# One deformable-convolution and attention kernel: image 0's sampling in turn with the other images' offsets

## The chip, the core and the metric

The kernel runs on one core of one Trainium2 chip. The metric is device time in microseconds for one launch, as the median of several runs. One more execution was recorded by the hardware profiler, and all lines of the profile are of that execution.

A core has five engines that matter here. TensorE (PE in the profile, its weight loads PEld) multiplies matrices and also transposes. VectorE (DVE) does elementwise work and reductions. ScalarE (ACT) does activations and copies. GpSimd (POOL) does elementwise work and issues indirect transfers. SyncE (SP) issues transfers. Each engine carries out its own instructions in order; engines wait for each other at semaphores.

## The reference

Four images of 64 x 64 tokens and 256 channels in fp32 pass through two layers.

```python
# layer 0
g  = _gn(x)                                   # group norm, 32 groups
xp = g @ in_w + in_b                          # what is sampled
x1 = silu(batchnorm(depthwise3x3(g)))         # 256 channels
offset = x1 @ off_w + off_b                   # 8 groups x 9 points x (x, y)
mask   = softmax((x1 @ mask_w + mask_b).reshape(N, H, W, 8, 9), -1)
# each of the 9 points of a group is read bilinearly at its own place plus its offset,
# in xp with a border of one zero token, weighted by the mask, and the nine are added
x  = x + (samples * mask).sum(-1) @ out_w + out_b
# layer 1, on t = tokens of x
t = t + additive_attention(_ln_t(t))          # tanh(q[i] + k[j]) . Wa, softmax, weighted sum
t = t + half_capacity_ffn(_ln_t(t))           # feed forward for the upper half of the tokens
```

The offsets depend on the data, so where an image is read differs from token to token.

## The kernel before

The tokens of an image are cut into 32 tiles of 128. Layer 0 is computed in two stages that meet in memory outside the core.

**Offsets and weights** (`offsets_and_weights`, L263) is called once for all four images, in a scope of its own. For each image it has a *front* and then a loop over slabs; a slab is 8 tiles (`SLAB`), so there are four slabs an image.

- `front` loads the tokens (L336 on), turns them to channels on PE (L339), counts their statistics on DVE (L341), copies them into a padded image `xn` with ACT (L342) and normalises it there (L366). The front of the next image is stepped through within the slabs of this one.
- `convolution` computes the depthwise 3 x 3 convolution. Channel chunk 1 goes through PE as nine matmuls by diagonal matrices (L420), chunk 0 through DVE as nine multiply-adds (L432, L434). ACT applies batch norm and SiLU (L424, L435). A slab's convolution is issued ahead of the taps of the slab before.
- `taps` multiplies by the weights of offsets and masks (L444), DVE takes the result out of PSUM (L448) and begins the softmax (L456, L457).
- `window` ends the softmax (L463 to L465), makes three hat functions of each offset on ACT (L473 to L477), and the largest absolute offset of each token (L476). With these, DVE spreads the nine points' bilinear weights over a 5 x 5 window of fixed shifts: for each of 3 x 3 hats a product (`my` L483, `mxy` L486) and an addition into `w5` (L488), which POOL has set to zero (L480). PE turns the result (L497), ACT copies it (L499), and SP stores it in `wt`.
- `projection` computes `xp` for 16 image rows (L387, L392), stores it in `xp` (L398), and turns it back into a table of token pairs `tab` (L405 to L407). SP issues all these transfers.

Then the **pads**: zero rows above and below `xp` and `tab` of each image are stored from a zero tile `zm`, which POOL clears (L1393), by 24 transfers on SP (L1398, L1399).

Then **`sample_image(0, 6)`** (L672) runs alone. First `list_tokens` (L534) lists the tokens with an offset too large for the 5 x 5 window. For each of 4 token chunks of 1024 and 2 channel chunks, it loads a stretch of `xp` (`xs`, L687) and, for each of 25 shifts, a row of weights broadcast over partitions (`wb`, L692, 512 KB). DVE multiplies (L701) and adds (L709). With depth 6 there are 12 buffers for `wb` and two each for `xs`, `ac`, `prd`. In between, `exact_rows` (L567) computes listed tokens exactly with indirect transfers issued by POOL (L630). After each token chunk come the output projection (PE, L725), the bias on POOL (L729), the addition on DVE (L732) and the store of `t` (L733).

Then the loop over images: for each, attention's preparation (`attention_prep`, L787, which first loads `t` into `v`, L774) in turn with the feed forward of the image before and the sampling of the image after, and then attention itself. There, sampling has depth 1: two buffers of `wb`, one each of the others.

The order within a stage is set by the tile framework's scheduler, with priorities by the order in which the program issues instructions; `keep` holds an instruction to program order on its engine, and `pinned` does so for every operation of DVE that is called through it. The generators' `yield`s are the points at which the program goes from one stage to the other; `S.left` counts the steps that are left in sampling.

Of the kernel before, what the change touches and what calls it, by code (L numbers as in the profile page):

```python
# [45 lines left out]
def layers_kernel(ctx: ExitStack, tc: tile.TileContext, a, out: bass.AP):  # L46
# [207 lines left out]
    class Pinned:  # L254


        def __getattr__(self, name):
            op = getattr(nc.vector, name)
            return lambda *args, **kw: keep(op(*args, **kw))  # L259

    pinned = Pinned()

    def offsets_and_weights(images, slab, rows_bufs):  # L263

        ca = S.a_one
# [52 lines left out]
        diag = ca.tile([P, K2, P], F32, name="diag")  # L318
        for tap in range(K2):
            nc.vector.tensor_scalar(diag[:, tap], ident, dwk[:, 1, tap : tap + 1], None, ALU.mult)  # L320

        def front(n):

            xn = S.a_xn.tile([P, CC, PITCH, PITCH], F32, tag="xn", name="xn")
            for k in range(CC):
                for e in (0, PITCH - 1):
                    nc.gpsimd.memset(xn[:, k, e, :], 0.0)
                    nc.gpsimd.memset(xn[:, k, :, e : e + 1], 0.0)

            st = S.a_sm.tile([P, CC, 8, 6], F32, tag="st", name="st")  # L330
            for s in range(8):
                xt = S.a_ld.tile([P, 4, C], F32, tag="xt", name="xt")
                nc.sync.dma_start(
                    out=xt, in_=x_d[n, s * 512 : (s + 1) * 512].rearrange("(t p) c -> p t c", p=P)
                )
                for k in range(CC):  # L336
                    pt = S.a_t.tile([P, 4, P], F32, tag="pt", name="pt")
                    for t in range(4):
                        nc.tensor.transpose(pt[:, t, :], xt[:, t, k * P : (k + 1) * P], ident)  # L339
                    ptf = pt.rearrange("p t q -> p (t q)")  # L340
                    nc.vector.bn_stats(st[:, k, s, :], ptf)  # L341
                    nc.scalar.copy(  # L342
                        xn[:, k, 1 + 8 * s : 9 + 8 * s, 1 : 1 + W],
                        ptf.rearrange("p (r w) -> p r w", w=W),
                    )
                yield
            mv = S.a_sm.tile([P, CC, 2], F32, tag="mv", name="mv")
            for k in range(CC):
                nc.vector.bn_aggr(mv[:, k, :], st[:, k].rearrange("p s f -> p (s f)"))

            gavgf = gavg.rearrange("p a b -> p (a b)")
            pg = S.a_t.tile([P, CC], F32, tag="pt", name="pg")
            nc.tensor.matmul(pg, gavgf, mv[:, :, 0], start=True, stop=True)
            gm = S.a_sm.tile([P, CC], F32, tag="gm", name="gm")
            nc.vector.tensor_copy(gm, pg)
            gv = S.a_sm.tile([P, CC], F32, tag="gv", name="gv")
            nc.vector.tensor_sub(gv, mv[:, :, 0], gm)
            nc.vector.tensor_mul(gv, gv, gv)
            nc.vector.tensor_add(gv, gv, mv[:, :, 1])
            pg2 = S.a_t.tile([P, CC], F32, tag="pt", name="pg2")  # L360
            nc.tensor.matmul(pg2, gavgf, gv, start=True, stop=True)
            gr = inv_std(S.a_sm, pg2, CC, "gr")
            nc.vector.scalar_tensor_tensor(gm, gm, -1.0, gr, ALU.mult, ALU.mult)
            for k in range(CC):
                inner = xn[:, k, 1 : 1 + H, 1 : 1 + W]
                nc.scalar.activation(inner, inner, AF.Identity, bias=gm[:, k : k + 1], scale=gr[:, k : k + 1])  # L366
            xns[n] = xn
# [3 lines left out]
        for _ in front(images[0]):  # L371
            pass
        for at, n in enumerate(images):
            xn = xns.pop(n)
            after = front(images[at + 1]) if at + 1 < len(images) else iter(())
# [4 lines left out]
            def projection(s):  # L380
                xp = xps[s % len(xps)]
                for h in range(2):
                    for f in range(CC):
                        pm = S.a_m.tile([P, 8, W], F32, tag="pm", name="pm")
                        r0 = 16 * s + 8 * h
                        for k in range(CC):
                            nc.tensor.matmul(  # L387
# [9 lines left out]
                for f in range(CC):  # L397
                    nc.sync.dma_start(out=xp_d[n][f][:, q0 : q0 + 16 * MP], in_=xp[:, f, : 16 * MP])  # L398
                for o in range(0, 16 * MP, P):
                    m = min(P, 16 * MP - o)  # L400
                    pt = S.a_t.tile([P, 2, CC, P], F32, tag="pt", name="ptc")
                    tb = S.a_ld.tile([P, CC, GH, 2, CG], F32, tag="tb", name="tb")
                    for c in range(2):
                        for f in range(CC):
                            nc.tensor.transpose(pt[:m, c, f, :], xp[:, f, o + c : o + c + m], ident)  # L405
                        nc.scalar.copy(tb[:m, :, :, c, :], pt[:m, c].rearrange("p f (e g) -> p f g e", g=GH))
                    nc.sync.dma_start(out=tabw[q0 + o : q0 + o + m], in_=tb[:m].rearrange("p f g c e -> p (f g c e)"))  # L407


            x1s, raws = {}, {}  # L410

            def convolution(s):
# [3 lines left out]
                for o in range(0, slab * P, 512):  # L416
                    pc = S.a_m.tile([P, 8, W], F32, tag="pm", name="pc")
                    for tap in range(K2):
                        r = r0 + o // W + tap // 3
                        nc.tensor.matmul(  # L420
                            pc, diag[:, tap], xn[:, 1, r : r + 8, tap % 3 : tap % 3 + W],
                            start=(tap == 0), stop=(tap == K2 - 1),
                        )
                    nc.scalar.activation(  # L424
                        x1[:, 1, o : o + 512], pc.rearrange("p r w -> p (r w)"), AF.Silu,
                        bias=bnsh[:, 1:2], scale=bns[:, 1:2],
                    )
                acc = x1[:, 0].rearrange("p (r w) -> p r w", w=W)
                for tap in range(K2):
                    src = xn[:, 0, r0 + tap // 3 : r0 + tap // 3 + 2 * slab, tap % 3 : tap % 3 + W]  # L430
                    if tap == 0:
                        nc.vector.tensor_scalar(acc, src, dwk[:, 0, 0:1], None, ALU.mult)  # L432
                    else:
                        nc.vector.scalar_tensor_tensor(acc, src, dwk[:, 0, tap : tap + 1], acc, ALU.mult, ALU.add)  # L434
                nc.scalar.activation(x1[:, 0], x1[:, 0], AF.Silu, bias=bnsh[:, 0:1], scale=bns[:, 0:1])  # L435

            def taps(s):
                x1 = x1s.pop(s)
                raw = S.a_wk.tile([P, slab, 3 * GP], F32, tag="raw", name="raw")
                for t in range(0, slab, 2):  # L440
                    po = S.a_m.tile([P, 2, 3 * GP], F32, tag="pm", name="po")
                    for j in range(2):
                        for k in range(CC):
                            nc.tensor.matmul(  # L444
# [3 lines left out]
                    nc.vector.tensor_tensor(  # L448
# [7 lines left out]
                nc.vector.tensor_reduce(red, m3, AX.X, ALU.max)  # L456
                nc.vector.tensor_tensor(m3, m3, rbc, ALU.subtract)  # L457
# [3 lines left out]
            def window(s):  # L461
                raw, m3, red, rbc = raws.pop(s)
                nc.vector.tensor_reduce(red, m3, AX.X, ALU.add)  # L463
                nc.vector.reciprocal(red, red)
                nc.vector.tensor_tensor(m3, m3, rbc, ALU.mult)  # L465
# [10 lines left out]
                nc.vector.tensor_reduce(omax[:, n, s * slab : (s + 1) * slab], hat[:, 1], AX.X, ALU.max)  # L476
# [3 lines left out]
                nc.gpsimd.memset(w5, 0.0)  # L480
                for ey in range(3):
                    my = S.a_w1p.tile([P, slab, GP], F32, tag="my", name="my", bufs=2)
                    nc.vector.tensor_mul(my, raw[:, :, 2 * GP :], hat[:, ey, :, GP:])  # L483
                    for ex in range(3):
                        mxy = S.a_w1p.tile([P, slab, GP], F32, tag="mxy", name="mxy", bufs=2)
                        nc.vector.tensor_mul(mxy, my, hat[:, ex, :, :GP])  # L486
                        blk = w5[:, :, ex : ex + 3, ey : ey + 3]
                        nc.vector.tensor_tensor(  # L488
                            blk, blk, mxy.rearrange("p t (g i j) -> p (t g) i j", i=3, j=3), ALU.add
                        )  # L490

                w5t = w5.rearrange("p (t f g) i j -> p t f (g i j)", t=slab, f=CC)
                for t in range(0, slab, 4):
                    for f in range(CC):
                        pt = S.a_t.tile([P, 4, P], F32, tag="pt", name="ptw")
                        for j in range(4):
                            nc.tensor.transpose(pt[: GH * ND, j, :], w5t[:, t + j, f, :], ident)  # L497
# [3 lines left out]
                        nc.sync.dma_start(out=wt_d[n][f, :, o : o + 512], in_=wT[: GH * ND])  # L501

            ns = NT // slab
            convolution(0)
            for s in range(ns):
                if s + 1 < ns:
                    convolution(s + 1)
                taps(s)
                window(s)
                for i in range(s * (H // 16) // ns, (s + 1) * (H // 16) // ns):  # L510
                    projection(i)
                for _ in range(8 // ns):
                    next(after, None)
            for _ in after:
                pass
# [156 lines left out]
    def sample_image(n, depth=1):  # L672
# [8 lines left out]
        single = exact_rows(n, uf, exact)  # L681
        for c in range(L // CH):
            ac = S.dn.tile([P, CC, CH], F32, tag="ac", name="ac", bufs=min(depth, 2))
            for f in range(CC):
                xs = S.dn.tile([P, CH // W + 4, MP], F32, tag="xs2", name="xs2", bufs=min(depth, 2))
# [4 lines left out]
                for d in range(ND):  # L690
                    wb = S.dn.tile([P, CH], F32, tag="wb", name="wb", bufs=2 * depth)
# [6 lines left out]
                    else:  # L698
                        prt = S.dn.tile([P, CH], F32, tag="prd", name="prd", bufs=min(depth, 2))
# [5 lines left out]
                    S.left -= 1  # L705
                    own = S.gather and next(single, None)
# [5 lines left out]
                    while own:  # L712
                        own = next(single, None)
                        S.left -= 1
                        yield
            for i in range(0, CH // P, 2):
# [765 lines left out]
```

## Time and profile before

| what | value |
|---|---|
| median of 3 runs | 10574.97 us (10574.79 to 10576.85) |
| profiled execution | 10547.94 us |
| its span, from first to last recorded instruction | 10546.2 us |
| mean granted TensorE clock | 0.916 of full speed |
| DVE receives the first constant, `inw` (L269) | 30.10 us |
| first convolution on DVE (L432) | 55.16 us |
| first eviction of taps (L448) | 93.45 us |
| `zm` cleared (L1393) | 811.48 us |
| last pad issued (L1399) | 841.64 us |
| first product of image 0's sampling (L701) | 868.28 us |
| first load of `v` in attention's preparation (L774) | 1485.75 us |

The first part of the profile's page gives busy time by engine: PE 9022.3 us (86% of the span), DVE 8536.6 (81%), ACT 7374.7 (70%), POOL 5276.0 (50%). Its second part cuts the span into 40 equal slices of 264 us; a digit is the busy share of a slice in tenths, and the row `PEclk` the clock that the throttle granted to TensorE. The view of windows gives the same quantities for stretches that one chooses. The view of groups has one row for each kind of instruction: its line, engine, operation, output and inputs with their sizes, count; then busy time and the mean duration of one in ns; then idle time of the engine just before them, and what ended most of it. The timeline has one row for an instruction: its start, its duration in us, and in brackets how long its engine was idle before it and for what.

### The profile page before, as it was taken

Reading aid. Unit: us, or ns where it says so; the run is one execution under the profiler, and the core shown is the slowest. Engines: PE = TensorE matmul, PEld = TensorE weight load, DVE = VectorE, ACT = ScalarE, POOL = GpSimd, SP = SyncE. Lnnn points to the kernel's source line nnn. Section 1 sums busy time; section 2 is a strip of 40 time slices with the busy share of each in tenths; the row PEclk is TensorE's granted clock in tenths of the full one; section 3 lists DMA queues with packets and bytes.
Section 4 is the critical chain, followed back from the end, with each engine's and each line's share of the span. In section 5 each row is a group of like instructions: output and inputs, shape, how many; then the busy total and the mean of one; then the engine's idle time right before and its main releaser. Section 6 shows DMA issues by size and latency. Waiting matters only on the chain. (4 is left out here: it accounts for less than half of the span.)

```text
span 10546.2 us, 115935 instructions
## 1 busy us (share of the span) xinstructions
PE 9022.3 (86%) x38460; PEld 4384.6 (42%) x38460; DVE 8536.6 (81%) x13342; ACT 7374.7 (70%) x8389; POOL 5276.0 (50%) x3059
## 2 busy tenths in 40 slices
PE   7881039999999788999999689999999699999995
PEld 4541014444444343444444344444444344444443
DVE  7776879898989778989899679899898367777772
ACT  4450018888888537888888438888888379999991
POOL 0004207676555326767655327677555155555552
PEclk8995569999999888999999789999999799999997
DMA  3336642222212252212111342122111300000002
GB/s 120 108 137 184 206 164 70 61 67 61 70 64 74 95 168 63 52 54 58 53 55 51 115 154 53 53 53 55 52 57 43 101 13 9 10 8 7 7 5 75
DMA packets 381329, 766.00 MB, mean 73 GB/s; under 512 B 49104, under 2 KB 212592, under 8 KB 380688
## 3 DMA queue, kind: packets, MB, share of 16 engines
q1 hardware_dynamic: 324432, 678.78, 19.7%
q0 software_dynamic: 30144, 45.87, 2.8%
q10 hardware_dynamic: 26112, 33.56, 0.9%
q8 instruction: 309, 5.06, 0.2%
q14 instruction: 332, 2.72, 0.1%
HBM read 580.88 MB, written 177.14 MB: 72 GB/s over the span
## 5 line engine op out<-in xcount | busy, mean ns | idle before, releaser
L913 DVE TENSOR_TENSOR r<-nn,r 128x512 f32<-128x512 f32 x6144 | 3937.1, 681 | 862.2 <-PE nn L908 805.6
L908 PE MATMUL nn<-qn,kf 32*128 32x512 f32 (+1 forms) x12288 | 4518.9, 640 | 131.9 <-DVE r L913 95.7
L998 POOL TENSOR_TENSOR r<-r 128x1024 f32<-128x1024 f32 x1024 | 2709.6, 2646 | 2635.7 <-DVE r L913 2623.6
L992 ACT ACTIVATE r<-d 128x1024 f32<-128x1024 f32 x3072 | 3114.0, 1014 | 1089.0 <-DVE r L1002 693.3
L898 PE MATMUL d<-qf,kf 32*128 32x512 f32 (+1 forms) x12288 | 3341.3, 632 | 77.2 <-DMA qf<-qf 43.0
L994 ACT ACTIVATE r<-r 128x1024 f32<-128x1024 f32 x3072 | 3124.1, 1051 | 32.7
L908 PEld LDWEIGHTS nn<-qn,kf 32*128 32x128 f32 (+1 forms) x12288 | 1399.4, 185 | 1896.4 <-DVE r L913 1443.2
L936 PE MATMUL pv<-v,et 128*128 128x257 f32 x8192 | 2107.1, 401 | 15.0 <-DVE acv L960 15.0
L936 PEld LDWEIGHTS pv<-v,et 128*128 128x128 f32 x8192 | 1509.9, 194 | 980.5 <-issue 772.8
L898 PEld LDWEIGHTS d<-qf,kf 32*128 32x128 f32 (+1 forms) x12288 | 1018.1, 186 | 1340.3 <-issue 725.1
L1000 POOL TENSOR_TENSOR r<-r 128x512 f32<-128x512 f32 x1024 | 1332.7, 1301 | 95.8 <-DVE r L913 20.6
L701 DVE TENSOR_TENSOR prd<-xs,wb 128x1024 f32<-128x1024 f32 x768 | 974.5, 1269 | 51.2 <-DMA wb<-wt 48.2
L709 DVE TENSOR_TENSOR ac<-ac,prd 128x1024 f32<-128x1024 f32 x768 | 996.2, 1297 | 8.8
L630 POOL DMA_INDIRECT ga<-tab,tii x576 | 727.1, 1262 | 208.2 <-issue 116.3
L920 ACT ACTIVATE et<-et,nshift 128x512 f32<-128x512 f32 x1024 | 723.9, 707 | 28.2 <-DVE et L1005 28.2
L1002 DVE TENSOR_TENSOR r<-r 128x512 f32<-128x512 f32 x1024 | 720.9, 704 | 4.1 <-POOL r L998 3.7
L1005 DVE TENSOR_TENSOR et<-r 128x512 f32<-128x512 f32 x1024 | 695.7, 679 | 0.4
L115 ACT ACT_TABLE_LOAD x9 | 11.5, 1283 | 797.9 <-DVE mv L259 700.0
L725 PE MATMUL pmo<-outwp,ac 128*128 128x256 f32 x512 | 136.1, 416 | 469.6 <-DVE ac L709 431.9
L480 POOL MEMSET w<- 128x1600 f32 x16 | 22.9, 1432 | 674.3 <-DVE red L456 386.4
L725 PEld LDWEIGHTS pmo<-outwp,ac 128*128 128x128 f32 x512 | 100.9, 205 | 522.1 <-DVE ac L709 305.1
L420 PE MATMUL pc<-xn,diag 128*128 128x512 f32 x576 | 262.6, 610 | 33.4 <-ACT xn L366 33.4
(344 smaller groups left out, 5278.9 us busy)
## 6 DMA issues: line engine op xcount, KB each, us to landing
wb<-wt SPq DMA_DIRECT2D x800, 512.0 KB
tab<-tb SPq DMA_DIRECT2D x128, 256.0 KB
v<-t SPq DMA_DIRECT2D x64, 512.0 KB
xs<-xp SPq DMA_DIRECT2D x32, 680.0 KB
xp<-xp SPq DMA_DIRECT2D x32, 544.0 KB
xt<-in_x_dram SPq DMA_DIRECT2D x32, 512.0 KB
xr<-in_x_dram SPq DMA_DIRECT2D x64, 256.0 KB
t<-xr SPq DMA_DIRECT2D x64, 256.0 KB
```

The lines of the kernel that those rows point to most:

```text
L630: keep(nc.gpsimd.indirect_dma_start(out=ga[:, s, dy].rearrange("p c e -> p (c e)"), out_offset=None, in_=tab_d[n], in_offset=bass.Indirect ...
L701: keep(nc.vector.tensor_tensor(pr.rearrange("p (r w) -> p r w", w=W), src, wb.rearrange("p (r w) -> p r w", w=W), ALU.mult,))
L709: keep(nc.vector.tensor_add(ac[:, f, :], ac[:, f, :], pr))
L898: keep(nc.tensor.matmul(d[:, j, :], kf[g, blk, rows(kt)], qs[q][0][g, blk, :], start=True, stop=True))
L908: keep(nc.tensor.matmul(nn, kf[g, blk, rows(kt)], qs[q][1][g, blk, :], start=True, stop=True))
L913: keep(nc.vector.tensor_tensor(r[:, j, :], ns[j], r[:, j, :], ALU.mult))
L920: keep(nc.scalar.activation(ets[b], ets[b], AF.Exp, bias=nshift))
L936: keep(nc.tensor.matmul(pv, ets[b0 + i][:, rows(j)], v[:, k0 + i, :], start=(i == 0), stop=(i == PVB - 1)))
L992: keep(nc.scalar.activation(rs[b, p], ds.pop((b, p)), AF.Ln))
L994: keep(nc.scalar.activation(rs[b, p], rs[b, p], AF.Exp, scale=-1.0))
L998: keep(nc.gpsimd.tensor_tensor(rs[b, 1], rs[b, 1], rs[b, 2], ALU.add))
L1000: keep(nc.gpsimd.tensor_tensor(rs[b, 1][:, 0], rs[b, 1][:, 0], rs[b, 3][:, 0], ALU.add))
```

## The change

The pads come first, and their transfers are issued by ACT's queue instead of SP's. Then one scope holds both the offsets stage and image 0's sampling. `offsets_and_weights` becomes a generator with slabs of 4 tiles (eight an image). It runs through image 0 up to its last slab, and from there on yields five times a slab. At the five yields of a slab, sampling of image 0 advances by 4, 4, 4, 3 and 3 steps.

Within the offsets:

- PE's and DVE's operations are all held to program order.
- The next image's front is cut into steps (`turned`, `counted`, `means`, `variances`, `normalised`), which are placed at fixed points of the slabs.
- For images 1 to 3, channel chunk 0 of the convolution goes through PE too, with nine more diagonals; image 0 keeps it on DVE.
- `w5` is cleared by DVE instead of POOL.
- A slab's weights are turned and stored (`turn`) at the end of the next slab.
- The projection of 16 rows is cut in two, at table block 5, one half a slab.
- The stores of `xp`, `tab` and `wt` are issued by ACT's queue instead of SP's.
- Buffers: `a_ld` 3 to 2, `my`, `mxy` and `xp`'s tile 2 to 1, `a_t` and `a_m` 4 to 3 PSUM banks each; `ps_m` takes the other two.

In sampling of image 0: `wb` has 2 buffers instead of 12, `prd` and `xs` 1 instead of 2, `ac` 2. The output matmuls of a chunk are put off into the next chunk, two at every eighth shift, and the additions of their results one such place later (`outputs`). Sampling of images 1 to 3 is as before. From the first load of `v` on, each engine's instructions stand in the same order in both kernels. Only image 1's `list_tokens`, which the scheduler had put on DVE between 814 and 833 us, now stands between the steps of attention's preparation for image 0.

```diff
+        vec, pe = pinned, Pinned(nc.tensor)
-        diag = ca.tile([P, K2, P], F32, name="diag")
-        for tap in range(K2):
-            nc.vector.tensor_scalar(diag[:, tap], ident, dwk[:, 1, tap : tap + 1], None, ALU.mult)
+        diag = ca.tile([P, CC, K2, P], F32, name="diag")
+        for k in (1, 0):
+            for tap in range(K2):
+                nc.vector.tensor_scalar(diag[:, k, tap], ident, dwk[:, k, tap : tap + 1], None, ALU.mult)
...
+            steps = {}
+            for s in range(4):
+                steps[s] = tuple(
+                    functools.partial(f, 2 * s + h) for f, h in ((turned, 0), (turned, 1), (counted, 0), (counted, 1))
+                )
+            nothing = lambda: None
+            steps[4] = nothing, lambda: of_group(mv[:, :, 0]), means, nothing
+            steps[5] = nothing, lambda: of_group(gv), variances, nothing
+            steps[6] = nothing, nothing, normalised, nothing
+            return steps
...
-                    nc.sync.dma_start(out=xp_d[n][f][:, q0 : q0 + 16 * MP], in_=xp[:, f, : 16 * MP])
+                    nc.scalar.dma_start(out=xp_d[n][f][:, q0 : q0 + 16 * MP], in_=xp[:, f, : 16 * MP])
                 for o in range(0, 16 * MP, P):
+                    if o == 5 * P:
+                        yield
...
+                for k in range(CC):
+                    if k == 0 and not at:
+                        acc = x1[:, 0].rearrange("p (r w) -> p r w", w=W)
...
+                        continue
+                    for o in range(0, slab * P, 512):
+                        pc = S.a_m.tile([P, 8, W], F32, tag="pm", name="pc")
+                        for tap in range(K2):
+                            r = r0 + o // W + tap // 3
+                            pe.matmul(
+                                pc, diag[:, k, tap], xn[:, k, r : r + 8, tap % 3 : tap % 3 + W],
+                                start=(tap == 0), stop=(tap == K2 - 1),
+                            )
...
-                nc.gpsimd.memset(w5, 0.0)
+                w5s[s] = w5
+                vec.memset(w5, 0.0)
...
-                        nc.sync.dma_start(out=wt_d[n][f, :, o : o + 512], in_=wT[: GH * ND])
+                        nc.scalar.dma_start(out=wt_d[n][f, :, o : o + 512], in_=wT[: GH * ND])
...
+        for i in range(len(images) * ns):
+            at, s = divmod(i, ns)
+            if s == 0:
+                cur = ahead
+                after = front(images[at + 1]) if at + 1 < len(images) else {}
+            one, two, three, four = after.get(s, nothing)
+            cur.taps(s)
+            one()
+            if s + 1 < ns:
+                cur.convolution(s + 1)
+            elif at + 1 < len(images):
+                ahead = image(at + 1)
+                ahead.convolution(0)
+            if at:
+                yield
+            window = cur.window(s)
+            three()
+            next(window)
+            if at:
+                yield
+            two()
+            if s % 2 == 0:
+                rows16 = cur.projection(s // 2)
+                next(rows16)
+            else:
+                next(rows16, None)
+            if last:
+                last[0].turn(last[1])
+            last = cur, s
+            for _ in range(3):
+                next(window)
+                if at:
+                    yield
+            four()
+            if at == 0 and s == ns - 1:
+                yield
+        last[0].turn(last[1])
...
-    def sample_image(n, depth=1):
+    def sample_image(n, sums=1):
...
+        def outputs():
+
+            while adds:
+                adds.pop(0)()
+            for _ in range(min(2, len(late))):
+                adds.append(late.pop(0)())
...
-                    wb = S.dn.tile([P, CH], F32, tag="wb", name="wb", bufs=2 * depth)
+                    wb = S.dn.tile([P, CH], F32, tag="wb", name="wb", bufs=2)
...
-    with scope(
-        ("a_one", 1, 0), ("a_xn", 2, 0), ("a_ld", 3, 0), ("a_wk", 2, 0), ("a_w1p", 1, 0), ("a_sm", 2, 0),
-        ("a_t", 4, 1), ("a_m", 4, 1),
-    ):
-        offsets_and_weights(range(NB), SLAB, 2)
     with scope(("one", 1, 0)):
...
-                    nc.sync.dma_start(out=xp_d[n][f][:, q0 : q0 + 2 * MP], in_=zm[:, : 2 * MP])
-                nc.sync.dma_start(
+                    nc.scalar.dma_start(out=xp_d[n][f][:, q0 : q0 + 2 * MP], in_=zm[:, : 2 * MP])
+                nc.scalar.dma_start(
...
-    with scope(("smp", 2, 0), ("two", 2, 0), ("sb", 2, 0), ("dn", 1, 0), ("ps_m", 2, 1)):
-        for _ in sample_image(0, 6):
+    with scope(
+        ("a_one", 1, 0), ("a_xn", 2, 0), ("a_ld", 2, 0), ("a_wk", 2, 0), ("a_w1p", 1, 0), ("a_sm", 2, 0),
+        ("smp", 2, 0), ("two", 2, 0), ("sb", 2, 0), ("dn", 1, 0), ("a_t", 3, 1), ("a_m", 3, 1), ("ps_m", 2, 1),
+    ):
+        others = offsets_and_weights(range(NB), SLAB // 2, 1)
+        next(others)
+        first = sample_image(0, 2)
+        for at, _ in enumerate(others):
+            for _ in range((4, 4, 4, 3, 3)[at % 5]):
+                next(first, None)
+        for _ in first:
             pass
```

## The prediction

> **What bounds the kernel now.** The span is 10546.2 us of a profiled execution of 10547.94 us, so 1.7 us lie around it; the median, 10574.97, is 27 us more, and I carry differences over to it. I began with the page's 40 slices (264 us each): after the start, up to slice 6, the busy engine changes.
>
> ```profile
> PE   7881039999999788999999689999999699999995
> DVE  7776879898989778989899679899898367777772
> ACT  4450018888888537888888438888888379999991
> PEclk8995569999999888999999789999999799999997
> ```
>
> Slices 1 to 3 have PE at 0.7 to 0.8, slices 4 to 6 have PE at 0.1, 0 and 0.3, ACT at 0 and the clock at half: first all four images' offsets, then image 0's sampling alone. From the first load of `v` (L774) at 1485.75 us on, the order of instructions is the same in both kernels. So the change is worth what it does to the stages before that. Their busy times (columns: us; busy us of PE, PEld, DVE, ACT, POOL with counts; granted clock; DMA share; GB/s):
>
> ```profile
> 0.00:61.00 61.00, 19.39 (x83) 15.32 (x84) 45.09 (x143) 21.44 (x24) 18.75 (x52) 0.87 0.38 115
> 61.00:812.00 751.00, 628.95 (x2378) 376.70 (x2377) 536.24 (x708) 365.68 (x627) 22.70 (x31) 0.90 0.35 123
> 812.00:868.00 56.00, 29.75 (x136) 29.31 (x136) 19.11 (x71) 0.00 (x0) 0.43 (x1) 0.50 0.55 187
> 868.00:1478.00 610.00, 44.56 (x134) 32.86 (x134) 510.80 (x463) 0.00 (x0) 205.31 (x162) 0.53 0.64 191
> ```
>
> The offsets are bound by PE (629 of 751 us, DVE 71%), the sampling by DVE (511 of 610, PE 7%); 56 us between them are pads and image 0's list. PE and DVE limits added one after the other: that is the room. In the offsets DVE spends (groups of that window: busy, mean ns, idle before):
>
> ```profile
> L434 DVE SCALAR_TENSOR_TENSOR x<-xn,dwk,x 128x1024 f32<-128x1024 f32 x125 | 159.3, 1275 | 2.6
> L488 DVE TENSOR_TENSOR w<-w,mxy 128x576 f32<-128x576 f32 x144 | 107.7, 748 | 0.4
> L486 DVE TENSOR_TENSOR mxy<-my,hat 128x576 f32<-128x576 f32 x144 | 102.6, 748 | 3.7 <-ACT hat L477 3.5
> L448 DVE TENSOR_TENSOR raw<-po,omb 128x432 f32<-128x432 f32 x64 | 37.6, 600 | 96.2 <-PE po L444 96.2
> ```
>
> And in the sampling, two instructions in turn:
>
> ```profile
> 1250.80 1.22 DVE L701 TENSOR_TENSOR prd<-xs,wb 128x1024 f32<-128x1024 f32 x1
> 1252.05 1.23 DVE L709 TENSOR_TENSOR ac<-ac,prd 128x1024 f32<-128x1024 f32 x1
> 1253.19 1.22 DVE L701 TENSOR_TENSOR prd<-xs,wb 128x1024 f32<-128x1024 f32 x1
> ```
>
> The pair repeats after 2.40 us (1253.19 less 1250.80).
>
> **Part 1: the start.** The pads' 24 DMAs took 29 us on SP (812.5 to 841.7) after the offsets. They now come first, on ACT's queue, and hold the zero tile; the scope of the offsets takes its place in memory, so `inw`, first in SP's queue there, waits for them. Behind `inw` on SP stand all constants and image 0's loads; DVE (L269) waits for it. It landed at 30.1 us. The zero memset stands on POOL behind the first constants, at about 28 us; pads end near 58, `inw` lands near 62.6: **+32 us**. From the first L432 (55.16) to the first `raw` eviction (L448, 93.45) the first convolution takes 38 us for eight tiles; for four I take 15 off, not 19, as the taps are still behind it; nine more diagonals to build on DVE add 3. So the first L448 comes at 93 + 32 - 15 + 3 = **113**. Bounds of this part: +5 if the pads overlap the building of constants, +35 without the shorter convolution.
>
> **Part 2: half slabs on DVE.** 128x576 takes 748 ns, 128x1024 1216 (L701): the line through both gives 448 ns at 128x288, and a dependent instruction starts 0.04 us after (1.26 pitch against 1.22): 0.49 us. Per slab of 4 tiles: L448 2 x 0.60; L456, L457, L463, L465 4 x 0.49; reciprocal 0.39; maximum 0.78 (half of 1345 and a fixed part); `my`, `mxy`, `w5` 21 x 0.49 = 10.3; the memset of `w5`, moved from POOL to DVE, 128x800. Its DVE duration isn't in the trace; POOL's row is 1.43 us for 1600 elements, so 0 to 1.4, and I take 0.85: 800 elements at the 1.04 ns that each adds between the two rows above. Sum **15.5 us**; a whole slab before costs 2 x 14, so halving costs about 3 us a slab.
>
> Here the skill speaks against the change: "VectorE: DVE Perf Modes", § The TRN2 errata, charges a fixed latency per instruction and advises tiles of 512 elements or more. Its table, 58 cycles + elements at 0.96 GHz, makes 360 ns of 288 elements, though it makes 660 of 576 where the row has 748. By the row 0.49 x 25 = 12.3 us a slab, by the table 10: over 24 slabs 53 us less. I take the row.
>
> **Part 3: what moves to PE.** Images 1 to 3 have channel chunk 0 of the convolution on PE too: per slab 9 more matmuls, 7.8 us by the pitch of L420's, in place of 2 x 0.64 x 5 on DVE. PE per slab: convolution 15.6, taps 3.0, projection 3.5/2, table about 3, weights 1.9, transposes 2.1: **27 us** at clock 0.90. ACT has 19 us, and 3 more for stores that it now issues in SP's place (0.32 us each by L407's row on SP); behind them wait the Silu and table copies, which PE needs later in the slab. SP is left with the loads and t's stores.
>
> **Part 4: image 0 alone, 8 slabs.** Its chunk 0 is still on DVE: 15.5 + 6.3 + 1.3 (statistics) = 23 us, PE and ACT in a chain of 27 and 23.5 in turn. About 25.5 a slab: **204 us** (113 to 317). Its list then takes 15: 332.
>
> **Part 5: sampling beside images 1 to 3, 24 slabs.** On DVE 24 x 15.5 + 32 x 0.69 (L341) + 5 = 398. Sampling: 192 x 2.40 + 8 x 1.14 = 470, the exact rows' sums (L641, L644) 28, output adds (L732) 11, rest 6: 515. Together **913 us**, 38 a slab; PE needs 27, so it is covered. What stood idle in the sampling before (42.7 us for `ga`, 43.2 at L732) is filled: gathers have 50 us now, and the adds come eight points late. New waits: `xs` has one buffer. Later in the kernel, where that is so already, it costs
>
> ```profile
> 3845.41 1.23 DVE L701 TENSOR_TENSOR ac<-xs,wb 128x1024 f32<-128x1024 f32 x1 [3.36 <-DMA xs<-xp]
> ```
>
> 3.4 us: seven times, 24. For DVE waiting on PE or ACT about 1.2 us a slab, 30; bounds 0 and 150. Behind a waiting pinned DVE instruction stands everything else on DVE, sampling and the next slab. So 332 + 913 + 54 = 1299, 7 us tail: `v<-t` near **1306**, 180 before 1485.75. Against it 9 us: image 1's list, which ran in the wait for the pads (814 to 833), now lies between the steps of attention's preparation. Net 171: **10405 us**.
>
> The other rule against it: "TensorE: Matmul & The Clock Gate", § Part 1: The HAM clock gate, halves the clock when an activity window of about 3.4 us is idle. PE idles 11 us of each 38. The rows show 0.90 at 84% busy and 0.53 at 7%; 70% lies between, nearer the first. By the rule a warm-up costs about 1.7 us a slab (estimate from the page), hidden in the slack. At half clock throughout PE would need 27 x 0.90/0.50 = 49 us a slab, 24 x 49 = 1176 and about 10615. I expect 0.8 or more.
>
> **Rivals.** *Bound by the chain (10490).* PE, ACT and DVE in fixed order with single `my`, `mxy` buffers and three PSUM banks: the 96 us at L448 and 40 at PE's ptw (L497) of the offsets stay as waits. At 42 us a slab instead of 40 with waits +50, at 44 +90. For it: these waits; against: 18 sampling steps stand between in each slab.
>
> *Better (10340).* The 30 us of waits vanish, the clock lets image 0 run at 23 us a slab (-20), the pads overlap (-15). For it: the sampling fills every hole.
>
> *Slower: the weights' broadcasts.* `wb` falls from 12 buffers to 2, 512 KB each, beside other stores. A pitch of (landing + 1.25)/2 for 200 of them passes 1138 us, the stage's break-even (967 + 171), at a landing of 10.1 us; at 12 it makes 1325 us and 10763. Against it: with two buffers, beside the feed forward,
>
> ```profile
> 3840.00:3900.00 60.00, 53.73 (x190) 34.82 (x189) 54.78 (x51) 20.62 (x27) 11.07 (x6) 0.94 0.64 213
> ...
> 3871.97 1.23 DVE L701 TENSOR_TENSOR prd<-xs,wb 128x1024 f32<-128x1024 f32 x1
> ...
> 3877.28 1.23 DVE L701 TENSOR_TENSOR prd<-xs,wb 128x1024 f32<-128x1024 f32 x1
> ```
>
> (window's row; then two uses of one buffer) the buffer free at 3873.20 is used at 3877.28: a load takes 4.1 us at most, at a DMA share of 0.64 and DVE 91% busy. In the new stage three quarters of the offsets' transfers (0.35 x 751 x 0.75) and the sampling's (0.64 x 610) make 588 of 967 us, 0.61.
>
> *No change:* the gain of part 5 is 171 only if both engines overlap; were all of it queued behind waits of 7 us a slab more, nothing would be left.
>
> **How the numbers follow.** Main case 0.60 (10365 to 10450), better 0.17, chain 0.17, no change 0.02, slower 0.04. The range runs from the better case with the table's cheaper instructions in part to the chain's end: 10310 to 10490. A measurement of this kernel tells about 0.2% (21 us) from no change. Faster: all of the first three, 0.94.
>
> **What would show it.** Pads before 60 us and first L448 near 113; `v<-t` near 1306; between, DVE above 90% busy with the clock at 0.8; `ga` waits gone; L488 at 128x288 near 450 ns; waits for `wb` few. Wrong if L448 or ptw keep DVE waiting over 4 us a slab, if the clock falls under 0.6, or if the rest after `v<-t` isn't 9060 us as now.

## The result, and the profile after

The changed kernel takes 10444.58 us (median of 4 runs, 10430.83 to 10450.11), the kernel before 10575.91 us beside it: a ratio of 0.9875, with a 95% interval of 0.9862 to 0.9887. That is 131 us less; 171 were forecast (10405), and the range of 10310 to 10490 holds it. The profiled execution took 10430.83 us, its span 10429.1. Most lines of the offsets stage now go through a helper, so the trace gives them as L263 and the tile names tell them apart. Old L701, L709, L692 and L774 are L828, L838, L819 and L893.

The 40 slices of the page, to be read beside the four rows of before:

```profile
PE   5777779999999589999999589999999699999995
DVE  5788979898989679899898689899898367777772
ACT  3333348887888438888888358888887389999991
PEclk8788879999999789999999789999999799999997
```

The hole in PE's and ACT's rows in slices 4 to 6 is gone. In slices 2 to 5 PE is at 0.7 and DVE at 0.7 to 0.9 together. The first load of `v`, from which on the order is the same, is this line of the timeline:

```profile
1361.46 8.97 SPq L893 DMA_DIRECT2D v<-t  x8
```

It stood at 1485.75 us; so 124 us are gained ahead of it. The stages ahead of it, by windows (columns as before): the rest of the start, image 0 alone, the token list with image 1's first taps, and the joint stage, in which image 0's sampling runs beside the offsets of images 1 to 3:

```profile
61.00:117.00 56.00, 27.23 (x93) 18.44 (x94) 24.06 (x61) 21.52 (x24) 2.82 (x4) 0.70 0.32 87
117.00:346.00 229.00, 184.70 (x601) 110.39 (x599) 166.62 (x328) 113.04 (x184) 1.14 (x8) 0.82 0.32 107
346.00:400.00 54.00, 41.39 (x158) 29.80 (x159) 21.69 (x77) 13.35 (x24) 5.25 (x6) 0.72 0.22 61
400.00:1361.00 961.00, 716.17 (x2236) 407.09 (x2234) 865.20 (x1191) 327.58 (x553) 181.95 (x166) 0.84 0.63 196
```

In the last row DVE is busy for 90% and PE for 75%, at a clock of 0.84. DVE's largest groups from 346 to 1358 us:

```profile
L828 DVE TENSOR_TENSOR prd<-xs,wb 128x1024 f32<-128x1024 f32 x192 | 237.9, 1239 | 10.8 <-DMA wb<-wt 6.3
L838 DVE TENSOR_TENSOR ac<-ac,prd 128x1024 f32<-128x1024 f32 x192 | 236.6, 1232 | 4.4
L263 DVE TENSOR_TENSOR mxy<-my,hat 128x288 f32<-128x288 f32 x216 | 101.8, 471 | 8.9
...
L263 DVE TENSOR_TENSOR raw<-po,omb 128x432 f32<-128x432 f32 x48 | 27.2, 599 | 18.6 <-PE po L263 18.6
```

and what DVE and PE waited for in the same 1012 us (view of waits: us in total, times, longest). `po` is the taps' result, `pl` the list's, `ptc` the transposes of a table block; all three are PE's. `tb` is ACT's copy of a table block:

```profile
DVE oh L647 <- PE pl L651: 20.6, 12, 15.1
DVE raw L263 <- PE po L263: 18.6, 9, 4.5
DVE ac L828 <- DMA xs<-xp: 12.7, 6, 3.3
DVE sT L749 <- PE pso L747: 11.6, 1, 11.6
...
PE ptc L263 <- ACT tb L456: 167.0, 125, 6.4
```

All of DVE's waits come to 93 us in 1012. For 167 us PE waits for ACT's copies of the table; the change holds PE's operations to program order.

### The profile page after: what moved, and what is told of

It is laid out like the page before. It is cut to its first block, busy times and chain, and to the rows that moved or that the text cites. A ratio compares the mean times of both kernels' runs of the same rounds, so it can differ in the third digit from the quotient of the medians.

```text
span 10429.1 us, 117382 instructions
## 1 busy us (share of the span) xinstructions
PE 9290.6 (89%) x38892; PEld 4512.6 (43%) x38892; DVE 8530.2 (82%) x13743; ACT 7464.3 (72%) x8525; POOL 5220.7 (50%) x3042
## 5 line engine op out<-in xcount | busy, mean ns | idle before, releaser
L1119 POOL TENSOR_TENSOR r<-r 128x512 f32<-128x512 f32 x1024 | 1330.5, 1299 | 98.3 <-DVE r L1032 23.1
L828 DVE TENSOR_TENSOR prd<-xs,wb 128x1024 f32<-128x1024 f32 x768 | 983.6, 1281 | 79.2 <-DMA wb<-wt 71.4
L838 DVE TENSOR_TENSOR ac<-ac,prd 128x1024 f32<-128x1024 f32 x768 | 990.9, 1290 | 6.6
L724 POOL DMA_INDIRECT ga<-tab,tii x576 | 698.6, 1213 | 353.8 <-DVE so L738 208.6
L263 PE MATMUL pc<-xn,diag 128*128 128x512 f32 x1008 | 452.2, 604 | 21.7 <-ACT xn L397 8.3
L788 POOL TENSOR_TENSOR xr<-xr,outb 128x512 f32<-128x512 f32 x64 | 88.1, 1381 | 551.4 <-DMA xr<-in_x_dram 486.1
L263 PE MATMUL ptc<-ident,xp 128*128 128x128 f32 (+1 forms) x576 | 136.9, 352 | 207.3 <-ACT tb L456 204.9
L263 PEld LDWEIGHTS pc<-xn,diag 128*128 128x128 f32 x1008 | 191.7, 193 | 257.2 <-issue 223.6
L456 ACT COPY tb<-ptc 128x256 f32<-128x256 f32 (+1 forms) x288 | 104.5, 370 | 240.7 <-PE ptc L263 132.4
```

What stands on the lines that cost most here:

```text
L828: keep(nc.vector.tensor_tensor(pr.rearrange("p (r w) -> p r w", w=W), src, wb.rearrange("p (r w) -> p r w", w=W), ALU.mult,))
L838: keep(nc.vector.tensor_add(ac[:, f, :], ac[:, f, :], pr))
L1119: keep(nc.gpsimd.tensor_tensor(rs[b, 1][:, 0], rs[b, 1][:, 0], rs[b, 3][:, 0], ALU.add))
```

## The experiments

Run again beside some of the experiments, the changed kernel took 10442.72 us and the kernel before 10558.1; "the control" below is that run (`after_again`). All other experiments had the kernel before at 10557 to 10561 us beside them. Since the stretch behind the first load of `v` lasted 9057 to 9092 us in these profiles with the same order of instructions, the place of that load is the sharper measure for what happens ahead of it.

> The changed kernel itself, for comparison on this chip: first taps at 118 us, list at 336, the first load of v at 1361 us, ratio to the kernel before 0.987 to 0.989.

Measured: the list's first instruction on DVE at 336.9, `v` at 1358.2, ratio 0.9887 (0.9870 to 0.9903). In the first profile of the changed kernel these stood at 336.6 and 1361.5.

**Is it the overlap? First attempt (`seq`).** No sampling between the yields:

```diff
         for at, _ in enumerate(others):
-            for _ in range((4, 4, 4, 3, 3)[at % 5]):
-                next(first, None)
+            pass
```

> All that the change does to the offsets stage stays; only the overlap is undone: image 0's sampling starts after the last slab of image 3. If the gain is the overlap, images 1 to 3 run alone at PE's pace, about 31 us of work and 5 of waits a slab (24 slabs: some 860 us after 346), then the list (30 to 50) and the sampling (about 560 to 600, still with two wb buffers): the first load of v near 1830 us instead of 1361, about 10900 us in all, slower than the kernel before by some 300 us. If the overlap gave little and the other edits gave the gain, it stays under 10600.

Measured: 10425.33 us in one run, `v` at 1340.7, earlier than in the changed kernel by 17 to 21 us. The overlap had not gone. DVE's timeline of this run:

```profile
559.50 1.22 DVE L828 TENSOR_TENSOR prd<-xs,wb 128x1024 f32<-128x1024 f32 x1
560.64 0.45 DVE L263 TENSOR_TENSOR mxy<-my,hat 128x288 f32<-128x288 f32 x1
561.01 1.22 DVE L838 TENSOR_TENSOR ac<-ac,prd 128x1024 f32<-128x1024 f32 x1
562.14 0.45 DVE L263 TENSOR_TENSOR w<-w,mxy 128x288 f32<-128x288 f32 x1
562.65 1.23 DVE L828 TENSOR_TENSOR prd<-xs,wb 128x1024 f32<-128x1024 f32 x1
```

The scheduler merged two chains of held instructions by itself, one of each in turn. A possible reason is that `keep` ties an instruction only behind the one that was issued just before it on its engine, while sampling's first held product stands behind the list's instructions, which aren't held. That is not tested; that the chain moved forward is seen. The merged order is also cheaper. The four instructions take 3.15 us here (562.65 less 559.50). In the changed kernel the product and the addition follow each other and wait for one another:

```profile
563.39 1.22 DVE L828 TENSOR_TENSOR prd<-xs,wb 128x1024 f32<-128x1024 f32 x1
564.64 1.23 DVE L838 TENSOR_TENSOR ac<-ac,prd 128x1024 f32<-128x1024 f32 x1
565.90 1.22 DVE L828 TENSOR_TENSOR prd<-xs,wb 128x1024 f32<-128x1024 f32 x1
...
568.31 0.46 DVE L263 TENSOR_TENSOR mxy<-my,hat 128x288 f32<-128x288 f32 x1
568.81 0.46 DVE L263 TENSOR_TENSOR w<-w,mxy 128x288 f32<-128x288 f32 x1
```

2.51 us for the pair, and two steps of 0.50 for `mxy` and `w`: 3.5 us. From the end of image 0's slabs to `v`, the changed kernel and then `seq`:

```profile
346.32:1361.46 1015.14, 757.57 (x2392) 436.89 (x2392) 886.57 (x1267) 340.88 (x577) 187.19 (x171) 0.83 0.61 189
344.21:1340.67 996.46, 751.65 (x2392) 438.63 (x2392) 825.94 (x1267) 341.12 (x577) 231.15 (x171) 0.84 0.62 193
```

DVE is busy for 61 us less with the same 1267 instructions. Most of this did not come through: its waits grew from 94 to 159 us in these stretches, those for PE's `po` from 18.6 to 46.7 and those for `wb` from 6.3 to 44.7.

**Is it the overlap? Second attempt (`two_scopes`).**

```diff
-        ("smp", 2, 0), ("two", 2, 0), ("sb", 2, 0), ("dn", 1, 0), ("a_t", 3, 1), ("a_m", 3, 1), ("ps_m", 2, 1),
+        ("a_t", 3, 1), ("a_m", 3, 1),
     ):
-        others = offsets_and_weights(range(NB), SLAB // 2, 1)
...
+        for _ in offsets_and_weights(range(NB), SLAB // 2, 1):
+            pass
+    with scope(("smp", 2, 0), ("two", 2, 0), ("sb", 2, 0), ("dn", 1, 0), ("ps_m", 2, 1)):
+        for _ in sample_image(0, 2):
             pass
```

> The overlap undone in earnest: the changed offsets stage of all four images in a scope of its own, then image 0's sampling (with the changed buffers and output order) in a second scope, so that its buffers exist only after the last slab. The run without steps between the yields kept the two stages in one scope, and its instructions were merged all the same. If the shared scope gives the gain: images 1 to 3 alone take 31 to 36 us a slab (740 to 860 us after 346), list and sampling 560 to 620; the first load of v at 1700 to 1840 us, and 10770 to 10910 us in all, slower than the kernel before, since half slabs and fixed orders cost what only the overlap pays for. If the other edits gave the gain, v comes before 1400 us.

Measured: 10929.34 us in one run, `v` at 1850.0. Its stages by windows, images 1 to 3 and then the sampling:

```profile
346.00:1180.00 834.00, 698.13 (x2258) 413.03 (x2258) 371.79 (x815) 342.77 (x573) 1.05 (x8) 0.87 0.25 88
1180.00:1900.00 720.00, 88.70 (x246) 61.97 (x246) 572.40 (x595) 20.40 (x37) 195.46 (x166) 0.53 0.61 179
```

PE is the bound of the first (84% busy), DVE of the second. So the edits around the overlap cost 364 us by themselves (1850 less 1486), and the shared scope gives back about 490 (1850 less 1358 to 1361). `seq` and `two_scopes` both issue the sampling last and differ in their scopes: 1340.7 against 1850.0. The shared scope, not the order written into the yields, carries the gain.

**Where are the 55 us that `v` came late? The list (`list_first`).**

```diff
         first = sample_image(0, 2)
+        next(first)
```

> One step of sampling, the token list, is issued before image 1's first slab instead of after its taps and convolution. Theory A (the list's matmuls stand in PE's queue behind the pinned convolution, and DVE's compare waits for them, 15 us at one place): the first product of sampling comes at about 365 to 375 us instead of 386 to 399, the first load of v 20 to 25 us earlier, about 10420 us. Rival: the list's ping-pong of DVE and PE costs the same wherever it stands, since it now holds up PE's convolution instead; then v and the time change by less than 8 us.

Measured: 10448.33 us; first product at 369.8 instead of 386, `v` at 1358.9, the control's place. The rival holds. In the changed kernel the list's matmuls did stand behind a convolution in PE's timeline:

```profile
365.22 15.62 PE L263 MATMUL pc<-xn,diag 128*128 128x512 f32 x36
380.68 4.52 PE L651 MATMUL pl<-tok,oh 128*128 128x2 f32 x28
```

but once that 15 us wait was gone, DVE waited longer elsewhere: 15.9 us for `wb` (6 to 7 before) and 25.9 for `po` (18 to 19 before).

**The table's transposes (`ptc_once`).**

```diff
                     for c in range(2):
                         for f in range(CC):
                             pe.transpose(pt[:m, c, f, :], xp[:, f, o + c : o + c + m], ident)
+                    for c in range(2):
                         nc.scalar.copy(tb[:m, :, :, c, :], pt[:m, c].rearrange("p f (e g) -> p f g e", g=GH))
```

> In the projection all four transposes of a table block are issued before its two copies, instead of two transposes, a copy, two transposes, a copy. Theory A (PE's fixed order makes it wait in place for the copy between the halves: 39 us for ACT's tb in image 0's slabs): those waits fall to under 15 us, the first sampling product comes 20 to 30 us earlier, v too; 10415 to 10425 us. Rival B (the copies are held by the stores that ACT issues between them, 0.33 us each, or by the two tb buffers): the waits stay above 25 us and the time changes by less than 10 us.

Measured: 10416.52 us (10409.26 to 10423.09), 26 less than the control. PE's wait for the table's copies in image 0's slabs (117 to 320 us), in the changed kernel and then in this run:

```profile
PE ptc L263 <- ACT tb L456: 36.2, 40, 4.0
```

```profile
PE ptc L263 <- ACT tb L457: 16.6, 14, 3.0
PE ptw L263 <- ACT tb L457: 6.8, 6, 2.3
```

The list begins at 315.9 instead of 336.6 us, `v` at 1340.2. The 21 us are gained in image 0's slabs; the joint stage is as long as it was (1024 us from the list's first instruction to `v` in both). Theory A holds for the gain. The waits it names fell to 16.6 us, a little above its 15, and 6.8 us of waits for the same copies appeared at `ptw` (the weights' transposes). So about 13 of the 21 us are waits that are gone; the granted clock of these 203 us rose from 0.82 to 0.87, and the rest is not followed here.

The kernel before has the same order of transposes and copies, but does not hold PE to program order. There PE waited far less for these copies; its first 1486 us and the changed kernel's first 1361:

```profile
L405 PE MATMUL ptc<-ident,xp 128*128 128x128 f32 x512 | 94.2, 306 | 24.3 <-ACT tb L406 22.5 <-ACT wT L499 1.0
```

```profile
L263 PE MATMUL ptc<-ident,xp 128*128 128x128 f32 x512 | 119.7, 346 | 181.9 <-ACT tb L456 180.4 <-DVE st L263 1.3
```

Other edits lie between the two rows as well, above all `a_t`'s PSUM banks, three instead of four, and no run undid one of them alone. So the share of the fixed order is open.

**The stores' queue (`stores_sp`).** The three `nc.scalar.dma_start` of `xp`, `tab` and `wt` are `nc.sync.dma_start` again.

> The stores of xp, tab and wt go back to SP's queue. Theory B (ACT's issues between the table copies slow the chain in image 0's slabs): image 0's eight slabs take 10 to 20 us less, and the time falls if the weights' loads on SP don't suffer. Theory A: no more than 8 us in image 0's slabs. Against both, in the joint stage a store that waits for its copy then stands ahead of weights' loads on SP: the waits of L828 for wb, 6 us now, grow to 20 to 100 us, and the whole is 10440 to 10540 us.

Measured: 10440.95 us, ratio 0.9886, as the control. Image 0's slabs end 4.5 us earlier (list at 332.1), so ACT's issues cost little there; in the joint stage DVE waits 34.4 us for `wb` instead of 6 to 7, and `v` comes at 1370.4, later by 9 to 12. The move to ACT's queue was worth about that much at `v`, below what the total resolves.

**The pads at the start (`pads_pool`).**

```diff
-    with scope(("one", 1, 0)):
-        zm = S.one.tile([P, 2 * G * 2 * CG], F32, name="zm")
+    with scope(("zero", 1, 0)):
+        zm = S.zero.tile([P, 2 * MP], F32, name="zm")
...
-                    nc.scalar.dma_start(out=xp_d[n][f][:, q0 : q0 + 2 * MP], in_=zm[:, : 2 * MP])
-                nc.scalar.dma_start(
+                    nc.gpsimd.dma_start(out=xp_d[n][f][:, q0 : q0 + 2 * MP], in_=zm)
+                nc.gpsimd.dma_start(
```

The scope of the zero tile stays open around the offsets and the sampling.

> The zero tile is 128 x 136 in a scope that stays open (the table's pads read it four times over), and its transfers are issued by POOL. If inw waits for the pads only through the tile's memory (step 1 of the prediction, +32 us): inw is received at about 30 us instead of 65, the first taps come at about 83 to 88 instead of 118, the first load of v about 30 us earlier, 30 us less in all. Rival: the 24 transfers or POOL's other work hold up the start anyway, or the joint stage gives the time back: less than 10 us.

Measured: 10406.01 us (10388.41 to 10411.52), 37 less than the control. The same instruction in the changed kernel and in this run:

```profile
65.44 0.70 DVE L278 COPY inwp<-inw 128x256 f32<-128x256 f32 x2 [39.01 <-DMA inb<-in_L_conv_in_b_dram]
```

```profile
28.88 0.69 DVE L278 COPY inwp<-inw 128x256 f32<-128x256 f32 x2 [2.93 <-DMA inw<-in_L_conv_in_w_dram]
```

In the changed kernel SP's queue, which issues `inw`, waits for the pads' transfers (view of waits, first 75 us):

```profile
SPq L70 <- DMA xp<-zm: 50.2, 2, 50.0
```

It issues `inw` at 62.47 us there and at 26.01 in this run. First taps come at 86.2 instead of 117.8, the list at 302.0 instead of 336.6, `v` at 1330.1: of the start's 32 to 35 us, 28 to 31 reach `v`.

**Both orders together (`seq_ptc`), and with the pads (`seq_ptc_pads`).**

> Both edits together: no sampling steps between the yields, and four transposes before the two copies of a table block. If they are independent (21 us each at the first load of v, one in the joint stage by DVE's alternation of independent instructions, one in image 0's slabs), v comes at about 1320 us and the time is 35 to 45 us below the changed kernel. If both only free DVE or PE to meet the weights' loads (waits of L828 for wb were 45 us without the steps), v stays near 1340.

Measured: 10358.58 us (10353.8 to 10363.64), `v` at 1273.0: 85 us before the control, not 38 to 42. The two are not independent. In `seq` alone PE waits 183.5 us in place for the table's copies and DVE in turn for PE's `po`; with four transposes in one go DVE's wait for `po` in the joint stage falls from 46.7 to between 5 and 6 us. This fits a stage in which the scheduler's order took DVE's limit down to PE's chain, and the transposes moved that chain.

Beside `ptc_once` this run also gives the plainest price of the order written into the yields: with the same transposes, leaving that order out brings `v` from 1340.2 to 1273.0 and the time from 10416.52 to 10358.58 us.

> The three edits together: no sampling steps between the yields, four transposes before the copies, pads out of the start's way. The pads' part lies in the start alone, which nothing overlaps: 28 to 31 us less than the run with the first two, the first load of v at about 1243 us, 10325 to 10335 us. If the start's gain is given back in the joint stage, it stays above 10350.

Measured: 10317.93 us (10313.74 to 10330.12), `v` at 1236.4. Ratio to the kernel before 0.9772 (0.9756 to 0.9788): it beats both kernels, the changed one by 125 us.

**Clearing on POOL (`mem_pool`, `seq_ptc_pads_mem`).**

```diff
-                vec.memset(w5, 0.0)
+                nc.gpsimd.memset(w5, 0.0)
```

> Against the changed kernel only the clearing of w5 goes back to POOL. It takes 24 x 0.72 us from DVE in the joint stage and 8 x 0.72 before it. If the joint stage is bound by DVE's work, the first load of v comes about 15 to 20 us earlier (1340 to 1345), some 15 to 20 us less in all. If waits take its place (the memset stands on POOL behind image 0's gathers, and DVE's additions wait for it), v changes by less than 5 us or comes later.

Measured: 10430.4 us, ratio 0.9879; `v` at 1351.8, 6 to 10 us earlier. It lies between both expectations. From the end of image 0's slabs to `v` DVE is busy for 873.8 us instead of 886.6, and its waits come to 99 us instead of 94; those for PE's `po` did not grow (17.7 against 18.6).

> The run with three edits and the clearing of w5 back on POOL. There DVE waits 49 us for the weights' broadcasts and 6 us for PE's taps; if what is left is bound by DVE's work, the first load of v comes 10 to 17 us earlier (about 1222 us), 10300 to 10310 us; if the broadcasts' landing or PE sets the pace, DVE's freed time goes into those waits, which grow by as much, and v stays within 5 us of 1236.

Measured: 10323.36 us, `v` at 1235.0. Nothing is gained. In the same stretch DVE is busy for 10 us less than in `seq_ptc_pads` (814.3 against 824.6), and its waits grow by 15 (127 against 112; `wb` 51.5 against 48.8, `po` 11.1 against 6.9).

**DVE or PE (`dve_conv`).**

```diff
-                    if k == 0 and not at:
+                    if k == 0:
```

> Channel chunk 0 of images 1 to 3 goes back to DVE (nine multiply-adds of 128x512 a slab, 6.3 us by image 0's rows of the changed kernel), nine matmuls (3.9 us at the pitch of 0.43) leave PE. If DVE bounds the joint stage, the first load of v comes about 24 x 6.3 = 150 us later, near 1505 us, and nothing of the change is left: 10570 to 10600 us. If PE's fixed chain bounds it, less than 60 us.

Measured: 10560.01 us in one run, `v` at 1469.9, about 110 us later, and the total that of the kernel before. From 400 to 1300 us:

```profile
400.00:1300.00 900.00, 502.99 (x1564) 302.61 (x1564) 840.49 (x1160) 281.37 (x463) 163.43 (x152) 0.72 0.57 173
```

DVE is busy for 93%, PE for 56%. The joint stage of the changed kernel is thus bound by DVE for the most part: 110 of the 150 us of added work come out at its end. Given the overlap, moving this convolution to PE was worth nearly the whole gain.

## Why the prediction came out right, and where its sum was off

**The shape was right.** DVE bounds the joint stage, PE is covered, and the overlap pays for the half slabs; `two_scopes` and `dve_conv` show it. By the two rows from 346 us on, PE is busy for 31.6 us a slab (757.6 / 24), where 27 were taken, and DVE for 37 (886.9 / 24). The gain is 77% of the forecast, and some of that is luck. `v` came 124 us earlier where 180 were forecast, and the two profiled executions differ by 117 us; the medians differ by 131, and executions of one kernel vary by 20 us and more.

**Part 1** held: `inw` was received at 65.4 us (+35, forecast +32), first taps at 117.8 (113). The cause is the tile's memory: SP's queue waits for the transfers that read `zm`, a tile that `inw` has nothing else to do with, and in `pads_pool`, whose zero tile keeps its memory, it does not. That run moves the pads to POOL's queue too, so it alone would not tell the two apart.

**Part 2** held: 128x288 takes 459 ns where the line through the trace gave 448 and the table of the Trainium skill's "VectorE: DVE Perf Modes", § The TRN2 errata, makes an estimate of 360; the memset takes 725 ns where 850 were taken.

**Part 4 failed in size:** "About 25.5 a slab: 204 us" is 28.6 us a slab and 228.5 us (117.8 to 346.3). The term left out is PE's wait in place for the table copies, 36 us; the change pins PE, and the transposes of a block alternate with its copies. `ptc_once` gets 21 of the 24.5 us back. The prediction listed PE and ACT as "in a chain" without asking what PE does between two halves of a block. The two figures of that chain, 27 and 23.5, are not worked out there: 27 is what Part 3 has for PE with both chunks, while image 0 has one of them on PE (23.1 us busy a slab, 184.70 / 8). It also counted the projection's matmuls at 3.5 us for 16 rows, as "3.5/2" a slab; they are 3.5 a slab.

**The list** took the 54 us from 346 to 400, together with image 1's first taps, where 15 were taken. `list_first` shows that it doesn't set the end.

**Part 5** was nearly right in its work and short in its waits. The 1012 us from 346 to 1358 hold 93 of waits and 919 of everything else (886 busy, 33 of gaps for which the view names no wait), where 913 of work, 15 for the list and 54 of waits were taken. Of the 93, some 26 are the list's (`oh`, `ls`, `pos`), and the 11.6 at `sT`, a step of the exact rows, were not thought of; the waits for `xs` are 12.7 us, not 24. In the work, one error is hidden: the pair of product and addition has a pitch of 2.51 us, not 2.40, or 21 us on 192 pairs. It is as long in `two_scopes`, where sampling runs alone as before:

```profile
1307.12 1.21 DVE L828 TENSOR_TENSOR prd<-xs,wb 128x1024 f32<-128x1024 f32 x1
1308.37 1.23 DVE L838 TENSOR_TENSOR ac<-ac,prd 128x1024 f32<-128x1024 f32 x1
1309.62 1.22 DVE L828 TENSOR_TENSOR prd<-xs,wb 128x1024 f32<-128x1024 f32 x1
```

The product starts 1.25 us after the addition, where 1.14 were enough in the prediction's lines (1252.05 to 1253.19). With one `prd` buffer instead of two the next product overwrites what that addition reads; no run gave the second buffer back. What made up for these 21 us was not followed, except for 3 us of the memset.

Added up at `v`: 1306 forecast, +5 from the start, +24 from image 0's slabs, +26 from the list and the joint stage's waits, 1361.

**The rivals.** The chain is part of what is missing, and in another place than it was given. It was to show at `raw` (old L448) and `ptw`; DVE's wait for `po` is 18.6 us in 24 slabs, 0.8 a slab. It cost 24 us in image 0's slabs instead, of which `ptc_once` shows 21. The 26 us of the list and the joint stage are spread over several waits, and no run assigns them. The slower case did not come: 6.3 us of waits for `wb` in the changed kernel. With the merged order they are 49 us, the largest wait that is left (`seq_ptc_pads`); more buffers were not tried. Half clock did not come either. The table of the Trainium skill's "TensorE: Matmul & The Clock Gate", § Part 1: The HAM clock gate, has two states, full and half; the mean over the joint stage is 0.84 at 75% busy, 0.72 at 56% (`dve_conv`), 0.53 at 12% (sampling in `two_scopes`). In these long stretches the mean goes with the busy share, as the prediction assumed from two rows; the 54 us of the list, at 77% busy and 0.72, do not fit.

**Open:** what image 1's list costs behind `v` (9 us forecast). The stretch behind `v` is 9060.4 us before and 9067.6 after in the first profiles of the two kernels, but 9057 to 9092 over all profiles with that order.

## What to carry to other kernels

When two stages with different bounds are overlapped, first ask what keeps the scheduler from merging them: here it was a scope of its own for each stage, and the order written by hand was worse than the one the scheduler found without it. An engine that is put in a fixed order waits in place, so look at each pair of instructions on it that has another engine's copy between them, and issue all of a block's inputs before its copies. A tile that is freed "before" a stage can still hold up the first load of that stage through its memory, as long as transfers read it. And a DVE that is busy for 90% can still have work to lose: here the order of its instructions alone was worth 61 us of it.

## What was not expected of the hardware

Dependent DVE instructions of 128x288 follow each other at 0.49 to 0.50 us, but an independent neighbour starts about 0.37 us after one of them (560.64 to 561.01 in `seq`). Alternating two chains took 3.15 us for four instructions that take 3.5 apart; over the 192 pairs of product and addition that would be some 65 us (192 x 0.35). DVE's busy time from the end of image 0's slabs to `v` fell by 61 us in `seq` and by 58 in `seq_ptc` beside `ptc_once` (826.5 against 884.9), without an instruction less. `v` came 67 us before `ptc_once`'s in `seq_ptc`; in `seq` alone, where DVE's waits grew, 17 to 21 us before the changed kernel's.
